# Moving an identity product one step later, with two PSUM banks given fixed names, in an edge-gated graph layer

## The chip, the cores and the metric

One Trainium2 chip, one core of it. The time is the device time of the whole program in microseconds (us). The kernel before was timed three times: 1103.55, 1104.61 and 1106.3 us, median 1104.61 us. One more execution was recorded by the hardware profiler; every duration of a single instruction comes from that one.

## The reference

`x` holds 16 graphs' node features (16 x 1024 x 256), `adj` is one sparse 1024 x 1024 matrix of edge weights, the same for all 16 graphs. For every graph:

```python
pre_u  = x @ W1[:256]                 # one row for each source node u
pre_v  = x @ W1[256:]                 # one row for each target node v
S      = sigmoid(relu(pre_u[:, :, None] + pre_v[:, None] + b1) @ W2 + b2)
a_t    = einsum('buv,bud->bvd', S * adj, x)
m_t    = einsum('uv,bud->bvd', adj, x) * x
z      = beta1 * x + beta2 * (a_t @ Wa + ba) + beta3 * (m_t @ Wm + bm)
```

Only the edges that `adj` really has are worked on. The output has the shape of `x`.

## The kernel before, in words

**Blocks and steps.** A block `k` is 128 target nodes of 4 graphs (8 node tiles times 4 groups of graphs: 32 blocks). Its edges are sorted into 10 lists of up to 128, five for each half of the 128 targets; one list is one step, so a block has `T = 10` steps and the program 320. The main loop (L886) runs over `n = 0 .. 321`, with `k, s = divmod(n, T)`: `s` is the step within the block. "Step 3" below means `s == 3`.

**What one edge list goes through.** GpSimd fetches, by an indirect DMA from a table in DRAM, the rows of the list's source nodes: `pre_u` and `x` of 4 graphs (L541, eight buffers `fetched`). TensorE spreads the targets' `pre_v` over the edges with a 0/1 matrix: `expand(n)`, two matmuls `pc<-X,mark` (L630). The PSUM tile `pc` has two buffers. VectorE adds the two (`add`, L665) and does relu, the product with W2 and the sum, once for each of the 4 graphs (`gate`, L673, with the accumulator read behind each). ScalarE makes the sigmoid (L676) and the weighted 0/1 matrices `left` (L678, L640). TensorE sums up over the edges: `aggregate(n)`, `acc<-fetched,left` (L690). Step `n` of the loop issues, in this order: VectorE's add for `n + 1`, its gate for `n`, and `expand(n + 2)`. The aggregates are issued two steps' worth at once, in the odd steps, for `n - 3` and `n - 2`.

**What is done once for a block, spread over steps.** Step 8, step 9, and steps 0 and 2 of the next block: `turn_over` (L700) transposes a quarter of the sums into a PSUM tile (`misc<-ident_r,ev`, L708) and ScalarE copies it into `LT` (L711). Steps 4 to 7 of the next block: `block_end` (L727) multiplies by Wa (steps 4 and 6, behind a matmul that writes the bias, L454) and by Wm (steps 5 and 7), and ScalarE copies the sum out (L744). Steps 1 and 3: the products of the next block's targets with W1[256:] (`L454` for b1, then eight matmuls L450 `misc<-w_v,hT`), two of the 4 graphs in each step; they become `X`, which the next block's `expand` needs from step 8 on.

**The two ways of making X.** `halves` (L496) splits `pre_v` into a rounded part and a rest on VectorE. `halves_turned` (L481), used for `turned(k)`, that is for blocks 2 to 11 and 24 to 31 (18 of 32), does it in PSUM: ScalarE writes the rounded, negated product into `X[:, 0]` (L489) and copies its upper half (L490); then a matmul with the identity adds that rounded part to the same PSUM tile `p`, so that the rest is left there (L492, the *identity product*); then two ScalarE instructions (L494) write the rest into `X`. So `p` stays occupied from its products until L494 is done. The generator is resumed by `go(parts, n)`: at the end of steps 1 and 3 for the products (L861), at the head of steps 3 and 5 for the identity products (L888).

**PSUM.** `pc` takes four banks, `acc0` and `acc1` one each. The other two are the pool `psm` (L219), two buffers under one name: every other PSUM tile comes from `small()` (L221) and gets one of the two; the tile allocated before in that bank must have been read to the end.

**What else lies on the way.** In blocks 0 to 4 `rows` (L457) makes the `pre_u` rows of group 1 (eight matmuls L450 `misc<-w_u,hT` for half of a tile, a copy L466, a DMA to the table one step later); `plan` (L801) says at which steps the tile's x is loaded and the two halves are made, and `rows` for groups 2 and 3 is planned further on. Until step 110 the edge lists of the tiles 4 to 7 are made by the generators `lists` (L243); their stages that use TensorE and a bank of `psm` say `"step"` and are put by `piece_of` and `fill` (L646, L657) between the other work, outside steps 1 to 6.

**Order.** The order of TensorE, VectorE, ScalarE, GpSimd and SyncE is the order in which the Python issues instructions (L515); each engine works through its own list in that order. The only freedom is how far one engine runs ahead of another.

Of the kernel before, what the change touches and what calls it, by code (L numbers as in the profile page):

```python
# [7 lines left out]
FP = mybir.dt.float32  # L8
# [5 lines left out]
P = 128  # L14
# [3 lines left out]
def kernel(  # L18
# [43 lines left out]
    B, N, D = x.shape  # L62
    NT = N // P
# [96 lines left out]
    same = hv.rearrange("p w q one -> p (w q) one").to_broadcast([P, NW * Q, V])  # L160
# [19 lines left out]
    slot, nth = upto, upto[:, :S]  # L180
# [26 lines left out]
    main = ctx.enter_context(ExitStack())  # L207
# [8 lines left out]
    lst = lst.enter_context(tc.tile_pool(name="lst", bufs=1))  # L216
    psc = main.enter_context(tc.tile_pool(name="psc", bufs=2, space=bass.MemoryType.PSUM))
    psa = main.enter_context(tc.tile_pool(name="psa", bufs=1, space=bass.MemoryType.PSUM))
    psm = main.enter_context(tc.tile_pool(name="psm", bufs=2, space=bass.MemoryType.PSUM))  # L219

    def small(name):  # L221
        return psm.tile([P, 512], FP, name="misc")


    def aside(vt):
# [17 lines left out]
    def lists(vt):  # L243
# [22 lines left out]
        cut = lst.tile([P, 1], FP, name="cut", bufs=2)  # L266
        nc.vector.tensor_reduce(cut, cand[:, :, 7], AX.X, ALU.max)
        yield "op"
# [93 lines left out]
        k_of = lst.tile([P, M], FP, name="k_of", bufs=2)  # L362
        nc.vector.tensor_reduce(k_of, eq, AX.X, ALU.add)
        yield "op"
# [33 lines left out]
    def count_rest():  # L398
        most = const.tile([P, 1], FP, name="most")
        nc.vector.tensor_reduce(most, longest, AX.X, ALU.max)  # L400
        nc.vector.tensor_copy(turns[:, :NT], longest)
# [45 lines left out]
    def half_product(p, hT, wt, h, begun):  # L447
        for bb in range(2):
            for i in range(DC):
                nc.tensor.matmul(p[:, bb * D:(bb + 1) * D], hT[:, 2 * h + bb, i, :], wt[:, i, :],  # L450
                                 start=(i == 0 and not begun), stop=(i == DC - 1), skip_group_check=begun)

    def add_row(p, parts):
        nc.tensor.matmul(p, unit, parts.unsqueeze(1).to_broadcast([P, 2, D]),  # L454
                         start=True, stop=False, skip_group_check=True)
# [22 lines left out]
    def turned(k):  # L478
        return 2 <= k <= 11 or k >= 24

    def halves_turned(k):  # L481
        X = cuts[k] = big.tile([P, NW, GD], FR, name="X")
        for h in range(2):
            yield
            c = slice(2 * h * D, (2 * h + 2) * D)
            p = small("p")
            add_row(p, b1_p)
            half_product(p, hTs[order[k]], w_v, h, True)
            nc.scalar.activation(X[:, 0, c], p, AF.Copy, scale=-1.0)  # L489
            nc.scalar.copy(X[W:, 1, c], X[W:, 0, c].bitcast(FP))  # L490
            yield
            nc.tensor.matmul(p, ident_r, X[:, 0, c], start=False, stop=True, skip_group_check=True)  # L492
            for w in range(NW):
                nc.scalar.activation(X[(1 - w) * W:(2 - w) * W, w, c], p[w * W:(w + 1) * W], AF.Copy, scale=-1.0)  # L494
# [23 lines left out]
    def do(step):  # L518
        for f in due.pop(step, ()):
            f()  # L520

    def go(gen, step):

        try:
            gen.send(step)
        except StopIteration:
            pass

    T = TW * NW

    BS = NG * NT
# [15 lines left out]
    def whole(pieces):  # L547
        return (said for said in pieces if said not in ("op", "slot"))

    made = [whole(lists(vt)) if vt < EARLY else lists(vt) for vt in range(NT)]  # L550
    turn = [(g, vt) for g in range(2) for vt in (*range(FIRST, NT), *range(FIRST))]
# [19 lines left out]
    def load_mark(q):  # L571
        marks[q] = big.tile([P, E], FR, name="mark")
        nc.scalar.copy(marks[q], whose[:, order[q // NW][1] * NW + q % NW, :])  # L573
# [9 lines left out]
    for t, turns_ in enumerate(script):  # L583
        step = t - 100
# [40 lines left out]
    def expand(n):  # L625
        k, g, vt, w, j = where(n)
        pcs[n] = psc.tile([P, GD], FP, name="pc")
        for h in range(2):
            c = slice(2 * h * D, (2 * h + 2) * D)
            nc.tensor.matmul(pcs[n][:, c], marks[n // TW][:, j * P:(j + 1) * P], cuts[k][:, w, c],  # L630
                             start=True, stop=True)
# [12 lines left out]
    running = []  # L644

    def piece_of(r, n):  # L646

        said = next(r[0], None)
        if said is None:
            running.remove(r)  # L650
        else:
            n += {"load": 4 if n else 7, "wait": 2, "slot": 1, "step": 1}.get(said, 0)
            while said == "step" and n > ROOM and 0 < n % T < 7:
                n += 1
            r[1:] = said not in ("slot", "step"), n

    def fill(n, gap=True):  # L657
        for r in running:
            if r[1] == gap and r[2] <= n:
                piece_of(r, n)  # L660
                break

    def add(n):
        t = fetched[at_slot[n]][:, :GD]
        nc.vector.tensor_tensor(t, t, pcs.pop(n), ALU.subtract if turned(n // T) else ALU.add)  # L665
# [126 lines left out]
    start_list = dict(zip((0, 14, 44, 72), range(EARLY, NT)))  # L792
    loads, at = {}, {}

    def plan(blocks, ns):

        for k, (load, *pieces) in zip(blocks, ns):
            loads[load] = k
            at.update((n, k) for n in pieces)

    plan(turn[NT:], ((0, 1, 8), (1, 9, 10), (9, 17, 18), (11, 19, 20), (19, 27, 28), (21, 29, 30), (29, 38, 39), (31, 40, 48)))  # L801
    for g, first in ((2, 60), (3, 140)):
        plan([(g, vt) for vt in range(NT)], ((first - 4 + 10 * i, first + 8 + 10 * i, first + (10 if first + 10 * i < 100 else 12) + 10 * i)
                                             for i in range(NT)))
# [62 lines left out]
    ROOM, MORE, LISTS = 10, 3, 110  # L867
# [9 lines left out]
    def gather_in(n):  # L877
        aggregate(n)
        free.append(at_slot.pop(n))
        refill()  # L880
        fetch_val(1 + (n % 3 == 0))
        if (n + 1) % TW in (0, MID + 1):
            half_end(n, 0 if (n + 1) % TW else 1)

    done = 0
    for n in range(total + 2):  # L886
        k, s = divmod(n, T)
        if s in (3, 5) and turned(k + 1) and k + 1 < BS:  # L888
            go(parts, n)
        if n < total - 3:  # L890
            last_in = n - 1 if n % 2 or n < ROOM else done
        else:
            last_in = n
        while done < min(last_in, total):
            gather_in(done)
            done += 1
        if n % TW == 1 and n // TW + 1 < total // TW:
            load_mark(n // TW + 1)
        if n < ROOM:
            if n + 2 < total:  # L900
                expand(n + 2)
            products(n, k, s)
        if n + 1 < total:
            add(n + 1)
        if n < total:
            gate(n)
            if n + 1 < total:
                left_adj(n + 1)
        do(n)
        if n >= ROOM and n + 2 < total:  # L910
            expand(n + 2)
        if n == 1:
            w_a = load_weights(Wa, "w_a", nc.sync)
            w_m = load_weights(Wm, "w_m", nc.sync)
            bias = load_rows(bm, D, "bias", nc.sync, spare[:, 1])
            ba_b = load_rows(ba, D, "ba_b", nc.sync, spare[:, 2])
            be1 = load_rows(beta1, 1, "be1", nc.sync)
            be2 = load_rows(beta2, 1, "be2", nc.sync)
            be3 = load_rows(beta3, 1, "be3", nc.sync)
            after(10, scale_late)  # L920
        if s in (5, 7) and k < BS - 1:
            h = s // 7
            hb = big.tile([P, 2, D], FP, name="h_blk", bufs=4)
            hbs.setdefault(k, []).append(hb)
            g, vt = order[k]
            nc.sync.dma_start(hb.rearrange("p b d -> p (b d)"),
                              table[g][vt * P:(vt + 1) * P, GD + 2 * h * D:GD + (2 * h + 2) * D])
        if n == total - 6:
            hbs[BS - 1] = hT_free.pop(0).rearrange("p b c n -> p b (c n)")
            for v, m, f in tails:  # L930
                for h, o in tail_rows(x, v, m, f):
                    nc.sync.dma_start(h, o)
        for i in advance.get(n, ()):
            next(made[i], None)
        if n in start_list:
            running.append([made[start_list[n]], True, n])
            piece_of(running[-1], n)
        fill(n, False)
        if n >= ROOM:
            products(n, k, s)  # L940
        if n == LISTS:
            assert not running and all(next(x, None) is None for x in made)
            lists_done()
            more = main.enter_context(tc.tile_pool(name="more", bufs=1))
            hT_free.extend(hT_places(more, MORE, NH))
        if n == 120:
            nc.gpsimd.partition_all_reduce(longest, rest, P, bass_isa.ReduceOp.max)
            after(n + 12, count_rest)
# [7 lines left out]
    with tc.If(any_left > 0):  # L956
        with ExitStack() as s2:
# [4 lines left out]
            for vt in range(NT):  # L962
# [17 lines left out]
                f = fb.tile([P, 2 * GD], FP, name="fb_f")  # L980
# [83 lines left out]
```

## Time and profile before

| | before |
|---|---|
| median of 3 runs | 1104.61 us |
| profiled execution: its time | 1116.06 us |
| its span, first to last instruction | 1114.2 us |
| around the span | 1.9 us |
| mean granted TensorE clock | 0.971 |
| TensorE (PE) busy | 1031.7 us |
| ScalarE (ACT) busy | 864.2 us |
| identity products (L492) | 36, mean 556 ns, 23.7 us of waits before them |
| L494 | 72, mean 592 ns |
| L489, L490 | 36 each, mean 588 ns and 616 ns |

PE is TensorE's matmuls, PEld its weight loads, DVE is VectorE, ACT is ScalarE, POOL is GpSimd, SP is SyncE. An instruction line of the timeline gives start, duration, engine, source line, operation, output and input with partitions x elements, how many are merged into the line, and in brackets the idle time of the engine just before and what ended it. Matmuls overlap in the pipeline: of two lines of PE, the distance of the starts is what the first one took of the engine.

### The profile page before, as it was taken

Reading aid. Unit: us, or ns where it says so; the run is one execution under the profiler, and the core shown is the slowest. Engines: PE = TensorE matmul, PEld = TensorE weight load, DVE = VectorE, ACT = ScalarE, POOL = GpSimd, SP = SyncE. Lnnn points to the kernel's source line nnn. Section 1 sums busy time; section 2 is a strip of 40 time slices with the busy share of each in tenths; the row PEclk is TensorE's granted clock in tenths of the full one; section 3 lists DMA queues with packets and bytes.
Section 4 is the critical chain, followed back from the end, with each engine's and each line's share of the span. In section 5 each row is a group of like instructions: output and inputs, shape, how many; then the busy total and the mean of one; then the engine's idle time right before and its main releaser. Section 6 shows DMA issues by size and latency. Waiting matters only on the chain.

```text
span 1114.2 us, 23979 instructions
## 1 busy us (share of the span) xinstructions
PE 1031.7 (93%) x7681; PEld 735.3 (66%) x7681; DVE 1006.8 (90%) x3469; ACT 864.2 (78%) x2639; POOL 460.8 (41%) x453
## 2 busy tenths in 40 slices
PE   7777898998999999899999999999999999999996
PEld 6654566765576667677677767676766666666663
DVE  8788887999999999899999999999999999999993
ACT  3346676777788888788898888988898888888873
POOL 2746643764346325634333434334333323333320
PEclk9979999998999999999999999999999999999999
DMA  9999998999999999999999999999999999998991
GB/s 286 335 379 335 312 323 282 397 343 374 340 373 377 384 382 371 357 387 382 404 409 389 404 384 388 388 402 392 348 374 359 354 328 337 350 368 333 341 352 42
DMA packets 149032, 394.56 MB, mean 354 GB/s; under 512 B 18224, under 2 KB 96048, under 8 KB 112688
## 3 DMA queue, kind: packets, MB, share of 16 engines
q0 software_dynamic: 50240, 300.11, 69.7%
q1 hardware_dynamic: 85360, 79.71, 22.5%
q10 hardware_dynamic: 13296, 13.11, 3.5%
q8 instruction: 63, 1.03, 0.4%
q14 instruction: 73, 0.60, 0.1%
HBM read 396.93 MB, written 50.33 MB: 401 GB/s over the span
## 4 chain that ended last, share of the span: by engine, by line
PE 55%; DVE 23%; ACT 12%; issue 7%; another core or an unknown queue 1%; DMA 1%; DVEq 0%; ACTq 0%
PE acc L690 14%; PE misc L739 13%; PE misc L450 12%; DVE fetched L673 12%; PE pc L630 9%; DVE fetched L665 7%; ACT left L678 4%; PE misc L708 2%; PE misc L454 2%; ACT mark L573 1%; ACT gt L676 1%; ACT LT L711 1%; ACT left L640 1%; ACT ev L698 1%; PE misc L492 1%
## 5 line engine op out<-in xcount | busy, mean ns | idle before, releaser
L541 POOL DMA_INDIRECT fetched<-table,uidx x320 | 342.7, 1071 | 557.8 <-PE acc L690 366.0
L673 DVE SCALAR_TENSOR_TENSOR fetched<-fetched,w_b 128x256 f32<-128x256 f32 x1280 | 476.9, 419 | 0.0
L665 DVE TENSOR_TENSOR fetched<-fetched,pc 128x1024 f32<-128x1024 f32 x320 | 388.5, 1214 | 62.1 <-PE pc L630 39.9
L678 ACT ACTIVATE left<-left,gt 128x32 f32<-128x32 f32 (+1 forms) x1280 | 299.5, 304 | 10.4
L690 PE MATMUL acc<-fetched,left 128*32 128x256 f32 x4096 | 268.0, 392 | 3.0 <-issue 1.6
L630 PE MATMUL pc<-X,mark 128*128 128x512 f32 x640 | 247.0, 467 | 7.3 <-DVE fetched L665 5.6
L690 PEld LDWEIGHTS acc<-fetched,left 128*32 128x32 f32 x4096 | 121.5, 111 | 108.4 <-issue 42.0
L630 PEld LDWEIGHTS pc<-X,mark 128*128 128x128 f32 x640 | 107.4, 192 | 85.5 <-issue 48.8
L676 ACT ACTIVATE gt<-sc,b_b 128x4 f32<-128x4 f32 x320 | 95.2, 298 | 79.4 <-DVE fetched L673 68.1
L739 PE MATMUL misc<-w_m,LT 128*128 128x256 f32 x496 | 119.1, 383 | 0.0
L739 PE MATMUL misc<-w_a,LT 128*128 128x256 f32 x496 | 117.2, 379 | 0.0
L450 PE MATMUL misc<-w_v,hT 128*128 128x256 f32 x448 | 110.3, 391 | 0.0
L739 PEld LDWEIGHTS misc<-w_m,LT 128*128 128x128 f32 x496 | 95.1, 192 | 15.5
L739 PEld LDWEIGHTS misc<-w_a,LT 128*128 128x128 f32 x496 | 93.8, 189 | 15.3 <-issue 0.3
L640 ACT ACTIVATE left<-onehot,val 128x64 f32<-128x64 bf16 (+1 forms) x320 | 102.9, 322 | 0.0
L673 DVE DVE_READ_ACCUMULATOR fetched<-fetched,w_b 128x1 f32 x1280 | 101.6, 79 | 0.0
L390 POOL DMA_INDIRECT val<-in_adjT_dram,vidx x80 | 87.7, 1096 | 32.4 <-issue 20.4
L450 PEld LDWEIGHTS misc<-w_v,hT 128*128 128x128 f32 x448 | 88.8, 198 | 14.8
L698 ACT COPY ev<-acc 128x512 f32<-128x512 f32 x128 | 74.7, 584 | 26.2 <-PE acc L690 13.9
L708 PE MATMUL misc<-ident_r,ev 128*128 128x128 f32 x512 | 78.9, 277 | 16.7 <-ACT low L506 9.4
L708 PEld LDWEIGHTS misc<-ident_r,ev 128*128 128x128 f32 x512 | 61.5, 141 | 40.3 <-ACT low L506 14.2
L711 ACT COPY LT<-misc 128x512 f32<-128x512 f32 x128 | 73.2, 572 | 8.5 <-remote 5.0
(184 smaller groups left out, 972.2 us busy)
## 6 DMA issues: line engine op xcount, KB each, us to landing
h_blk<-table SPq DMA_DIRECT2D x62, 256.0 KB
out_dram<-h_blk SPq DMA_DIRECT2D x62, 256.0 KB
hT<-in_xT_dram SPq DMA_DIRECT2D x28, 512.0 KB
table<-in_x_dram ACTq DMA_DIRECT2D x24, 512.0 KB
table<-tab SPq DMA_DIRECT2D x48, 256.0 KB
fetched<-table,uidx POOLq DMA_INDIRECT x320
table<-in_x_dram SPq DMA_DIRECT2D x8, 512.0 KB
table<-fetched SPq DMA_DIRECT2D x8, 512.0 KB
```

The costliest lines, as they stand in the source:

```text
L390: nc.gpsimd.indirect_dma_start(out=val[:, i, j:j + 1], out_offset=None, in_=adj_flat, in_offset=bass.IndirectOffsetOnAxis(ap=vidx[:, i, j: ...
L450: nc.tensor.matmul(p[:, bb * D:(bb + 1) * D], hT[:, 2 * h + bb, i, :], wt[:, i, :], start=(i == 0 and not begun), stop=(i == DC - 1), skip ...
L541: nc.gpsimd.indirect_dma_start(out=fetched[at_slot[n]], out_offset=None, in_=table[g], in_offset=bass.IndirectOffsetOnAxis(ap=uidx[:, vt * ...
L630: nc.tensor.matmul(pcs[n][:, c], marks[n // TW][:, j * P:(j + 1) * P], cuts[k][:, w, c], start=True, stop=True)
L640: nc.scalar.activation(lefts[n][:, :m, 1::GB, :], onehot[:, i, o:o + m, :].unsqueeze(2).to_broadcast([P, m, GB // 2, V]), AF.Copy, scale=v ...
L665: nc.vector.tensor_tensor(t, t, pcs.pop(n), ALU.subtract if turned(n // T) else ALU.add)
L673: nc.vector.scalar_tensor_tensor(t[:, b, :], t[:, b, :], 0.0, w2_b, ALU.max, ALU.mult, accum_out=sc[:, b:b + 1])
L676: nc.scalar.activation(gt, sc, AF.Sigmoid, bias=b2_b)
L678: nc.scalar.activation(lefts[n][:, :m, 2 * b, :], lefts[n][:, :m, 1 + b // 2 * GB, :], AF.Copy, scale=gt[:, b:b + 1])
L690: nc.tensor.matmul(accs[h][b * 2 * V:(b + 1) * 2 * V, r, :], left[:, i, 2 * b - b % 2:2 * b - b % 2 + 2].rearrange("p k v -> p (k v)"), f[ ...
L708: nc.tensor.transpose(pt[:, r, :, c, :], ev[:, r, c * P:(c + 1) * P], ident)
L739: nc.tensor.matmul(pz[:, bb * D:(bb + 1) * D], LTs[k][:, 2 * h + bb, i if bb else 1 - i, c, :], wt[:, c, :], start=False, stop=(i == 0 and ...
```

## The change

`small()` alternates between two names, `misc0` and `misc1`, each with one buffer, instead of leaving the choice of the bank to the pool; the second half's products of `halves_turned` ask for the name used last, which is that of the transpositions of step 2. Both identity products are issued behind both halves' products: the first at the head of step 4 instead of step 3, the second at the head of step 5 as before. The stages of `lists` that use a bank are held off steps 1 to 6 at the moment they would be issued, instead of when they become ready. The plan of the `rows` of group 1 is moved: no half is made in step 7 any more, the last one comes at step 50 instead of 48.

```diff
-    psm = main.enter_context(tc.tile_pool(name="psm", bufs=2, space=bass.MemoryType.PSUM))
-
-    def small(name):
-        return psm.tile([P, 512], FP, name="misc")
+    psm = main.enter_context(tc.tile_pool(name="psm", bufs=1, space=bass.MemoryType.PSUM))
+    bank = 0
+
+    def small(name, same=False):
+        nonlocal bank
+        bank ^= not same
+        return psm.tile([P, 512], FP, name=f"misc{int(bank)}")
...
     def halves_turned(k):
         X = cuts[k] = big.tile([P, NW, GD], FR, name="X")
+        ps = []
         for h in range(2):
             yield
             c = slice(2 * h * D, (2 * h + 2) * D)
-            p = small("p")
+            p = small("p", h == 1)
+            ps.append(p)
             add_row(p, b1_p)
             half_product(p, hTs[order[k]], w_v, h, True)
             nc.scalar.activation(X[:, 0, c], p, AF.Copy, scale=-1.0)
             nc.scalar.copy(X[W:, 1, c], X[W:, 0, c].bitcast(FP))
+        for h, p in enumerate(ps):
             yield
+            c = slice(2 * h * D, (2 * h + 2) * D)
             nc.tensor.matmul(p, ident_r, X[:, 0, c], start=False, stop=True, skip_group_check=True)
             for w in range(NW):
                 nc.scalar.activation(X[(1 - w) * W:(2 - w) * W, w, c], p[w * W:(w + 1) * W], AF.Copy, scale=-1.0)
...
-            while said == "step" and n > ROOM and 0 < n % T < 7:
-                n += 1
-            r[1:] = said not in ("slot", "step"), n
+            r[1:] = said not in ("slot", "step"), n, said == "step"
...
-            if r[1] == gap and r[2] <= n:
+            if r[1] == gap and r[2] <= n and not (r[3] and n > ROOM and 0 < n % T < 7):
...
-    plan(turn[NT:], ((0, 1, 8), (1, 9, 10), (9, 17, 18), (11, 19, 20), (19, 27, 28), (21, 29, 30), (29, 38, 39), (31, 40, 48)))
+    plan(turn[NT:], ((0, 1, 8), (1, 9, 10), (9, 18, 19), (11, 20, 28), (20, 29, 30), (29, 38, 39), (31, 40, 48), (40, 49, 50)))
...
-        if s in (3, 5) and turned(k + 1) and k + 1 < BS:
+        if s in (4, 5) and turned(k + 1) and k + 1 < BS:
             go(parts, n)
```

More of the change, by code (lines that the diff above doesn't have):

```diff
@@ L935 @@
         if n in start_list:
-            running.append([made[start_list[n]], True, n])
+            running.append([made[start_list[n]], True, n, False])
             piece_of(running[-1], n)
```

## The prediction

> **What bounds the kernel now.** I read the busy shares first, then the waits, then one late block as a table by stretches and as a timeline engine by engine.
>
> ```profile
> PE 1031.7 (93%) x7681; PEld 735.3 (66%) x7681; DVE 1006.8 (90%) x3469; ACT 864.2 (78%) x2639; POOL 460.8 (41%) x453
> ```
> Three engines are nearly full, so the bound lies in how they wait for each other. The waits, all engines:
>
> ```profile
> DVE fetched L665 <- PE pc L630: 39.9, 50, 2.1
> ...
> PE misc L492 <- ACT X L489: 23.7, 15, 2.8
> ```
> TensorE's largest wait, 23.7 us, stands before the identity product; the change is aimed at it. Which block it costs what is seen in block 27 (late, with no lists and no rows in it). One period of it, by stretches (busy us by engine):
>
> ```profile
> 943.81:973.07 29.26, 27.31 (x219) 18.98 (x218) 27.89 (x95) 25.31 (x81) 10.13 (x10) 1.00 0.96 348
> ```
> VectorE has 27.89 us of work in 29.26: it idles 1.37, nearly all in one place. TensorE's timeline of steps 2 to 5:
>
> ```profile
> 952.63 0.64 PE L708 MATMUL misc<-ident_r,ev 128*128 128x128 f32 x4
> 955.15 0.50 PE L492 MATMUL misc<-X,ident_r 128*128 128x512 f32 x1 [1.88 <-ACT X L489]
> 955.58 1.50 PE L690 MATMUL acc<-fetched,left 128*32 128x256 f32 x24
> 957.01 0.73 PE L630 MATMUL pc<-X,mark 128*128 128x512 f32 x2
> 957.82 0.50 PE L454 MATMUL misc<-b_p,unit 128*128 128x512 f32 x1
> 958.16 1.89 PE L450 MATMUL misc<-w_v,hT 128*128 128x256 f32 x8
> 959.70 0.81 PE L630 MATMUL pc<-X,mark 128*128 128x512 f32 x2
> 960.34 0.39 PE L454 MATMUL misc<-bias_p,unit 128*128 128x512 f32 x1
> 960.57 1.89 PE L739 MATMUL misc<-w_a,LT 128*128 128x256 f32 x8
> 962.11 0.58 PE L492 MATMUL misc<-X,ident_r 128*128 128x512 f32 x1
> 962.62 1.93 PE L690 MATMUL acc<-fetched,left 128*32 128x256 f32 x32
> 964.48 0.74 PE L630 MATMUL pc<-X,mark 128*128 128x512 f32 x2
> ```
> ScalarE and VectorE over the same time:
>
> ```profile
> 957.20 0.56 ACT L711 COPY LT<-misc 128x512 f32<-128x512 f32 x1
> 957.79 1.20 ACT L494 ACTIVATE X<-misc 64x512 fp32r<-64x512 f32 x2
> ...
> 960.40 0.60 ACT L489 ACTIVATE X<-misc 128x512 fp32r<-128x512 f32 x1
> 961.03 0.61 ACT L490 CAST X<-X 64x512 fp32r<-64x512 f32 x1
> ```
> ```profile
> 965.26 1.22 DVE L665 TENSOR_TENSOR fetched<-fetched,pc 128x1024 f32<-128x1024 f32 x1 [1.35 <-PE acc L690]
> ```
> Three things are to be seen. First, the second half's products start at 957.82, 0.06 after the copy L711 of step 2's transposition ends (957.76), and while L494 still reads the first half's tile (to 958.99): they already lie in the transpositions' bank. Naming the bank changes nothing. Second, the wait of 1.88 hides behind that: without it, these products still could not start before 957.76. Third, from there TensorE runs without a gap to the expand of step 5, ending at 965.22, and VectorE has waited 1.35 us for it. So one loop sets the period: gates on VectorE, ScalarE up to L711, TensorE from the second half's products to that expand, VectorE again. What lengthens the stretch 957.82 to 965.22 lengthens the block.
>
> **The change, part by part.**
>
> *Identity product from the head of step 3 to step 4, late blocks.* Removed: the wait of 1.88 and 0.43 of TensorE (955.15 to 955.58) in step 3. Two things are late next. The second list's aggregate needs `left`, ready at 954.38 (the four L678 that ScalarE began at 953.42); with 1.0 for its 16 matmuls and 0.57 for the expand TensorE gets to the products at about 956. There it waits for L711 until 957.76. Nothing is gained.
>
> Added in step 4, on the same clock. The products run 957.82 to 960.05 as before; TensorE takes the identity product at 959.70 (0.51, as 962.11 to 962.62), the expand at 960.21 (0.64), and could begin the Wa products (L454 at 960.34 above) at 960.85. But the bank was the transpositions' for the second half, so Wa's is the first half's, now held until its L494 pair has read it. ScalarE issues that pair behind the second half's L489 and L490: queued L489 (0.60), L490 (0.61), L494 (1.20), gaps 0.05. ScalarE is free at 960.05, since L494 no longer stands ahead of step 3's gate. So: 960.05 + 0.05 + 0.60 + 0.61 + 1.20 + 0.05 + 0.06 = 962.6. The wait is 1.75 to 1.8, and Wa starts 2.3 late (0.51 identity, 1.8 wait). Behind it TensorE has the second identity product, 32 aggregates and the expand that VectorE waits for: it ends at 967.5 instead of 965.22, VectorE's stall grows from 1.35 to 3.65, the period from 29.26 to 31.55. Bounds for this new wait, which the trace does not show: 0 if ScalarE were through by 960.85, 2.4 if the whole chain of 2.4 were bare. I take 1.8. Sum: 8 blocks (23 to 30) x 2.3 = **+18.4**.
>
> *The same in blocks 1 to 10.* Products again start 0.05 or 0.06 after L711 ends (201.88 after 201.83, 338.46 after 338.40, 405.49 after 405.44), so 2.3 is added there too, 23 in ten blocks. Less: blocks 1 and 5, where the waits of 2.84 and 1.87 did delay the products (1.0 and 1.25 past L711; the first estimated from the gates); blocks 2 and 3, where VectorE has list work and takes the expand 1.0 and 0.8 after it is ready (169.32 against 168.31; 210.05 against 209.28). 23 - 4.05 = **+19**.
>
> *Rows out of step 7.* At steps 17 and 27 the row products wait for the copies of a list's tile: 1.64 (on L294) and 2.99 (on L350), and run slowly behind it (L450 2.50 and 3.33 instead of 1.89, the Wm products 3.11 and 2.29 instead of 1.89): 4.6 + 3.7 = 8.3 at most. At least 0, or a loss of 2 if four halves in steps 8 to 0 each wait up to 0.5 for the Wm copy's bank (L744, 0.48 to 0.59); a fetch already ends one VectorE wait near there (1.26 at 151). I take **-6**, nearest to the rows with a cause. The moved loads still lead their rows by nine steps (some 27 us); the last table half leaves SP at step 51 instead of 49, and the first fetch from group 1 (step 60) is issued at 55. No cost seen there.
>
> *Hold on the lists' stages.* Same steps barred, tested later: 0, at worst one bank wait of 1 to 3.
>
> *Clock.* The granted clock in the stretch 894.13 to 897.5, behind a wait of 1.88, is 0.70 and 1.00 before. Four of the eight late blocks have it: their period is 30.51, +1.25. Seven of the 18 blocks show it in all. After the change each block has two gaps of about 1.8. None cold: -9; as often per block as late blocks now: +2.5; counted by gap: +14. I take **+5**.
>
> The Trainium skill, "TensorE: Matmul & The Clock Gate", section "HAM oscillation — how this bites in real kernels", asks only that no gap exceed some 3.4 us. By that rule the clock would cost nothing, here or before; the rows above show half-speed behind 1.88, so I go by them.
>
> The skill's "Perfetto Trace Analysis", section "Matmuls", says that independent groups should rotate through PSUM banks so that one's evacuation overlaps the next one's matmuls. It speaks against this change: two open halves take both banks at once.
>
> Sum: 18.4 + 19 - 6 + 5 = +36. The profiled execution, 1116.06 (span 1114.2 plus 1.9 around it), becomes 1152. It lies 11.5 over the median of the runs; the differences are the same there: 1104.6 + 36 = **1141 us**.
>
> **Rivals.**
>
> *Faster: the wait was the bound.* If L494 were done before TensorE gets to Wa, VectorE's stalls in step 6 go: 1.35 x 8 late blocks, about 1 x 10 early ones, 6 for the rows: 1104.6 - 27 = 1078. For it: the chain of waits that ended last does pass through L492 (955.15). Against: L711's end. It decides where ScalarE needs under 0.8 from the products' end (960.05) to L494's end; the rows give 2.4.
>
> *Absorbed early.* If the early blocks have slack everywhere (lists on VectorE, fetches), only the late ones pay and the rows give 8.3: 1104.6 + 18.4 - 8.3 = 1115. For it: blocks 2 and 3. Against: in blocks 6 to 10 VectorE waits 1.1 to 1.5 for the same expand.
>
> *Clock worse.* Both gaps make TensorE cold in every block: 36 x 1.25 less 7 x 1.25 = +36 in place of +5: 1172.
>
> **How the numbers follow.** Forecast 0.78 (1118 to 1160: per block 1.5 to 2.4, rows -8 to +2, clock -5 to +14), absorbed 0.08, faster 0.08, clock worse 0.06. The range 1112 to 1162 takes in the absorbed case. About 0.3% (3.3 us) is what a measurement can tell: faster 0.08, within 0.03 (part of the absorbed case), slower 0.89.
>
> **What would show it.** Right: L492's wait on L489 gone; waits of 1.7 on L711 before L454 in step 3 and 1.8 on L494 in step 4; late blocks at 31.5; VectorE's stall before L665 near 3.6 a block. Wrong: L454 in step 4 starting within 0.7 of the expand before it, or late periods under 29.3. The prediction fails if ScalarE does L494 ahead of the second half's L489.

## The result and the profile after

| | before | after |
|---|---|---|
| median, 4 runs each, same chip (us) | 1105.03 | 1138.2 (1135.78 to 1142.47) |
| ratio to before, with its 95% interval | | 1.0305 [1.027, 1.0339] |
| profiled execution: time, span (us) | 1116.06, 1114.2 | 1137.42, 1135.6 |
| mean granted TensorE clock | 0.971 | 0.980 |
| late block, shortest period (us) | 29.26 | 31.47 |

The change costs 33.2 us. The two profiled executions are only 21.4 us apart: before's lay 11 us above its median, over half of it from a late start (its first targets' products of step 1 in block 1 begin at 110.15; after's at 103.78, and those of the other kernels profiled between 102.9 and 104.9). That is not the change's doing, so medians give the size below and the profiles only the place. Ratios, here and below, go by the executions in the faster of two states alone, so a ratio need not be the quotient of the medians beside it.

In the new kernel the lines have moved: the bias product L454 is now L457, the identity product L492 is L499, its two ScalarE instructions L494 are L501, L489 and L490 are L494 and L495, the copy L711 is L716, the Wa and Wm products L739 are L744, VectorE's add L665 is L670. Busy time of after, from the top of its page:

```profile
PE 1031.6 (91%) x7681; PEld 731.1 (64%) x7681; DVE 1007.3 (89%) x3469; ACT 863.7 (76%) x2639; POOL 462.4 (41%) x453
```

No engine has noticeably more work than before (PE 1031.7, DVE 1006.8, ACT 864.2, POOL 460.8); the loss is waiting. The waits of after (who waited, for whom; total us, times, longest):

```profile
DVE fetched L670 <- PE pc L637: 87.3, 52, 4.1
...
PE misc L457 <- ACT X L501: 29.9, 18, 1.7
PE misc L457 <- ACT LT L716: 26.5, 18, 3.1
```

The identity product's 23.7 us of waiting on L489 have gone. In their place stand two waits in each of the 18 blocks: 29.9 / 18 = 1.66 on the first half's L501 in step 4, and 26.5 / 18 = 1.47 on the copy of step 2's transposition. VectorE's wait for the expand has grown from 39.9 to 87.3. TensorE in one late block, steps 3 to 5:

```profile
937.80 0.50 PE L457 MATMUL misc<-b_p,unit 128*128 128x512 f32 x1 [1.68 <-ACT LT L716]
938.14 1.89 PE L453 MATMUL misc<-w_v,hT 128*128 128x256 f32 x8
939.68 0.58 PE L499 MATMUL misc<-X,ident_r 128*128 128x512 f32 x1
940.10 0.63 PE L637 MATMUL pc<-X,mark 128*128 128x512 f32 x2
942.46 0.50 PE L457 MATMUL misc<-bias_p,unit 128*128 128x512 f32 x1 [1.74 <-ACT X L501]
...
946.71 0.73 PE L637 MATMUL pc<-X,mark 128*128 128x512 f32 x2
```

ScalarE over the same time:

```profile
937.18 0.56 ACT L716 COPY LT<-misc 128x512 f32<-128x512 f32 x1
...
940.07 0.60 ACT L494 ACTIVATE X<-misc 128x512 fp32r<-128x512 f32 x1 [0.30 <-PE misc L453]
940.70 0.61 ACT L495 CAST X<-X 64x512 fp32r<-64x512 f32 x1
941.22 1.19 ACT L501 ACTIVATE X<-misc 64x512 fp32r<-64x512 f32 x2
```

and VectorE's add for step 6, the instruction that the prediction followed:

```profile
947.48 1.22 DVE L670 TENSOR_TENSOR fetched<-fetched,pc 128x1024 f32<-128x1024 f32 x1 [3.61 <-PE pc L637]
```

Read them together. The second half's products start 0.06 after L716 ends (937.74), as they did after L711 before; the bank's name has bought nothing. The identity product and the expand pass through at once, and then TensorE stands from 940.72 to 942.46. ScalarE, from 940.07 on, does first the second half's L494 and L495, 1.15 us that the first half does not need, and only from 941.22 the L501 pair that frees the bank: the pair ends at 942.41, and L457 starts 0.05 later. The last expand ends at 947.44, and VectorE has waited 3.61 us for it where it waited 1.35. The period as a stretch, busy us by engine:

```profile
937.80:969.30 31.50, 28.09 (x219) 19.20 (x219) 27.87 (x97) 25.32 (x80) 10.04 (x10) 1.00 0.86 314
```

VectorE has 27.87 us of work in it, as before (27.89 in 29.26); the 2.24 us are added to its idle time.

### The profile page after: what moved, and what is told of

It reads as the page before. It is cut to its first block, busy times and chain, and to the rows that moved or that the text cites. A ratio compares the mean times of both kernels' runs of the same rounds, so it can differ in the third digit from the quotient of the medians.

```text
span 1135.6 us, 23998 instructions
## 1 busy us (share of the span) xinstructions
PE 1031.6 (91%) x7681; PEld 731.1 (64%) x7681; DVE 1007.3 (89%) x3469; ACT 863.7 (76%) x2639; POOL 462.4 (41%) x453
## 4 chain that ended last, share of the span: by engine, by line
PE 46%; DVE 22%; ACT 16%; DMA 9%; issue 6%; SPq 0%; POOL 0%; DVEq 0%; POOLq 0%; ACTq 0%
PE misc L744 13%; DVE fetched L678 11%; PE acc L695 11%; PE misc L453 10%; DVE fetched L670 8%; PE pc L637 6%; ACT left L683 4%; DMA table<-tab 4%; DMA fetched<-table,uidx 3%; PE misc L457 3%; ACT X L501 2%; ACT LT L716 2%; PE misc L713 1%; ACT X L495 1%; ACT gt L681 1%
## 5 line engine op out<-in xcount | busy, mean ns | idle before, releaser
L670 DVE TENSOR_TENSOR fetched<-fetched,pc 128x1024 f32<-128x1024 f32 x320 | 389.1, 1216 | 97.5 <-PE pc L637 87.3
L637 PE MATMUL pc<-X,mark 128*128 128x512 f32 x640 | 241.5, 459 | 9.4 <-DVE fetched L670 9.4
L744 PE MATMUL misc<-w_m,LT 128*128 128x256 f32 x496 | 117.6, 380 | 0.0
L744 PE MATMUL misc<-w_a,LT 128*128 128x256 f32 x496 | 117.2, 379 | 0.0
L453 PE MATMUL misc<-w_v,hT 128*128 128x256 f32 x448 | 114.2, 401 | 0.0
L744 PEld LDWEIGHTS misc<-w_a,LT 128*128 128x128 f32 x496 | 93.9, 189 | 14.6 <-ACT LT L716 0.4
L647 ACT ACTIVATE left<-onehot,val 128x64 f32<-128x64 bf16 (+1 forms) x320 | 102.9, 322 | 0.0
L744 PEld LDWEIGHTS misc<-w_m,LT 128*128 128x128 f32 x496 | 93.4, 190 | 14.6
L453 PEld LDWEIGHTS misc<-w_v,hT 128*128 128x128 f32 x448 | 90.8, 203 | 15.1
L716 ACT COPY LT<-misc 128x512 f32<-128x512 f32 x128 | 73.0, 571 | 3.0 <-PE misc L713 2.0
```

The lines of the kernel that those rows point to most:

```text
L647: nc.scalar.activation(lefts[n][:, :m, 1::GB, :], onehot[:, i, o:o + m, :].unsqueeze(2).to_broadcast([P, m, GB // 2, V]), AF.Copy, scale=v ...
L716: nc.scalar.copy(LT.rearrange("p b k c (r v) -> p r (b k c) v", v=V)[:, r:r + 2], pt.rearrange("p r k c v -> p r (k c) v"))
L744: nc.tensor.matmul(pz[:, bb * D:(bb + 1) * D], LTs[k][:, 2 * h + bb, i if bb else 1 - i, c, :], wt[:, c, :], start=False, stop=(i == 0 and ...
```

## The experiments

The ratios are to runs of the kernel before on the same chip, whose median was between 1102.8 and 1103.36 us in the three groups. "Early" is the stretch from the first targets' products of block 1 to those of block 11, "middle" from there to block 23, "late" from there to the second half's products in block 30.

| run | ratio [95%] | early, middle, late (us) | late period, shortest |
|---|---|---|---|
| before (its one profile) | 1 | 352.1, 368.4, 216.8 | 29.26 |
| after | 1.0305 [1.027, 1.0339] | 365.5, 365.3, 230.6 | 31.47 |
| e1 | 1.0018 [0.9985, 1.005] | 348.5, 364.5, 219.3 | 29.28 |
| e2 | 1.0325 [1.0261, 1.039] | | 31.49 |
| e3 | 1.0142 [1.008, 1.0204] | | 30.58 |
| e4 | 1.0572 [1.0497, 1.0646] | | 32.15 |
| e5 | 1.0052 [1.0021, 1.0083] | 346.7, 364.8, 221.1 | 30.05 |
| e6 | 0.9955 [0.9922, 0.9987] | 347.5, 364.8, 212.5 | 29.25 |
| e7 | 0.9931 [0.9904, 0.9957] | 335.5, 364.7, 213.0 | 28.91 |
| e11 | 0.9852 [0.9817, 0.9888] | 336.5, 368.3, 204.3 | 28.29 |
| e8 | 0.9896 [0.9859, 0.9933] | 342.9, 375.8, 204.2 | |
| e13 | 0.9998 [0.996, 1.0035] | 344.2, 365.9, 216.8 | 29.26 |
| e14 | 1.0023 [0.9995, 1.005] | 334.0, 391.9, 204.2 | |

The theory: the loss comes from the place of the identity products, through the bank that stays held behind ScalarE's queue. The rivals: the bank names, the new row plan, or the clock.

**e1: the identity products back, all else of the change kept.**

```diff
-        if s in (4, 5) and turned(k + 1) and k + 1 < BS:
+        if s in (3, 5) and turned(k + 1) and k + 1 < BS:
```
(and in `halves_turned` each half's identity product follows its own products again)

> The changed kernel with only the identity products put back to the heads of steps 3 and 5; bank names, lists' hold and row plan as changed. Theory (the first half's bank is held until ScalarE has read it behind the second half's copies, 2.3 us on the path of each of 18 blocks): all of the loss goes, and the row plan's gain of about 6 us shows: 1099 us, 1094 to 1106; late blocks 29.3 us apart again, no wait on L494's kind before the Wa products. Rival (strict alternation of two named banks or the moved rows cost it): it stays near 1138 us.

Measured 1104.78 us, ratio 1.0018 [0.9985, 1.005]. Names, hold and row plan together cost at most 0.5%, and the loss goes with the place. What was expected beyond that, a gain of some 4 us from the row plan, is not there. Late blocks are back at 29.3 us in one period of seven; in the other six they take 30.0 to 30.4, since six of the eight late blocks run partly at half the granted clock (last section).

**e2: the move alone.** The kernel before, with the split loop of `halves_turned` and steps (4, 5); the two-buffer pool, the old plan and the old hold stay.

```diff
-        if s in (3, 5) and turned(k + 1) and k + 1 < BS:
+        if s in (4, 5) and turned(k + 1) and k + 1 < BS:
```

> The kernel before with only the identity products moved behind both halves, to the heads of steps 4 and 5; the pool of two buffers chooses the banks, the row plan is the old one. Theory: the whole loss without the plan's gain, 1144 us (1138 to 1150); late blocks at 31.5 us; the pool chooses the same banks, so the same wait of about 1.75 us before the Wa products. Rival (names or plan make the loss): near 1105 us.

Measured 1141.95 us, ratio 1.0325 [1.0261, 1.039]: the whole loss, without one named bank. The waits of e2 are those of after (here L498 is the pair, L715 the copy):

```profile
PE misc L454 <- ACT X L498: 30.7, 18, 2.1
PE misc L454 <- ACT LT L715: 28.7, 18, 3.1
```

So the pool of two gives the second half the same bank by itself.

**e3: a shorter queue ahead of the release.** In the changed kernel the second half's rounded copy and its upper half are issued behind the first half's L501 pair (here L506) instead of ahead of it.

```diff
-            nc.scalar.activation(X[:, 0, c], p, AF.Copy, scale=-1.0)
-            nc.scalar.copy(X[W:, 1, c], X[W:, 0, c].bitcast(FP))
+            if h == 0:
+                rounded(p, c)
...
             for w in range(NW):
                 nc.scalar.activation(X[(1 - w) * W:(2 - w) * W, w, c], p[w * W:(w + 1) * W], AF.Copy, scale=-1.0)
+            if h == 0:
+                rounded(ps[1], slice(2 * D, 4 * D))
```
(`rounded(p, c)` is a new function that holds the two lines taken out)

> The changed kernel, with the second half's two ScalarE instructions (rounded copy and its upper half, 0.60 and 0.61 us) issued behind the first half's pair of reads instead of ahead of it. Theory: the queue on ScalarE is the price; the pair ends 0.05 + 1.20 us after the identity product, so the wait before the Wa products falls from 1.75 to about 0.7 us and late blocks from 31.5 to 30.4: 1120 us (1115 to 1126). Rival (the place of the identity product itself on TensorE is the price, 0.5 us and cold clock): no change, 1138 us.

Measured 1122.04 us, ratio 1.0142 [1.008, 1.0204], period 30.58. ScalarE and then TensorE of e3, late block:

```profile
936.88 1.19 ACT L506 ACTIVATE X<-misc 64x512 fp32r<-64x512 f32 x2 [0.52 <-PE misc L504]
938.10 0.60 ACT L489 ACTIVATE X<-misc 128x512 fp32r<-128x512 f32 x1
```
```profile
938.12 0.50 PE L457 MATMUL misc<-bias_p,unit 128*128 128x512 f32 x1 [0.82 <-ACT X L506]
```

The pair now starts as soon as the identity product has ended, and the wait falls from 1.74 to 0.82 with no work removed from ScalarE. What is left is the pair itself (1.19) less the part of the expand that runs beside it. Half of the loss was order on ScalarE; the other half is the identity product and its pair lying between two uses of one bank.

**e4: a longer queue.** The second half's upper-half copy is issued twice (the same data, a second time), so that 0.62 us more stand ahead of the pair.

```diff
-            nc.scalar.copy(X[W:, 1, c], X[W:, 0, c].bitcast(FP))
+            for _ in range(1 + h):
+                nc.scalar.copy(X[W:, 1, c], X[W:, 0, c].bitcast(FP))
```

> The changed kernel with the upper-half copy of the second half issued twice (0.62 us more on ScalarE ahead of the first half's pair of reads, same data). Theory: the wait before the Wa products grows by 0.62 us to about 2.35 in each of 18 blocks and late blocks to 32.1: 1149 us (1144 to 1153). Rival (ScalarE has room, 76% busy): no change, 1138 us.

Measured 1166.7 us, ratio 1.0572 [1.0497, 1.0646]. TensorE of e4 in a late block:

```profile
930.39 0.50 PE L457 MATMUL misc<-bias_p,unit 128*128 128x512 f32 x1 [2.39 <-ACT X L502]
930.73 3.51 PE L745 MATMUL misc<-w_a,LT 128*128 128x256 f32 x8
```

The wait is 1.74 + 0.65 = 2.39, and the one late period of seven in which the clock stays up is 32.15, 0.65 longer, as the queue's length says. But the other six are 33.75 to 35.48: at half the granted clock behind the gap of 2.39 the eight Wa products take 3.51 instead of 1.89. The direction and the wait were right; the size missed since the clock was left out of it.

**e5: the row plan alone**, in the kernel before.

```diff
-    plan(turn[NT:], (... (9, 17, 18), (11, 19, 20), (19, 27, 28), (21, 29, 30), (29, 38, 39), (31, 40, 48)))
+    plan(turn[NT:], (... (9, 18, 19), (11, 20, 28), (20, 29, 30), (29, 38, 39), (31, 40, 48), (40, 49, 50)))
```

> The kernel before with only the new plan of group 1's rows (none in step 7). The prediction gave the plan -6 us; the first run with the identity products put back showed no gain. Theory now: the two waits of step 7 go, but a table half is needed again two steps after its last use (steps 18 and 20, 38 and 40, 48 and 50), and ScalarE waits there for the DMA of the old one (2 to 6 us seen at three places): 1103 us, 1099 to 1107, waits of ScalarE's row copy on the table's DMA of 5 us or more in all. Rival (the plan gains and the bank names or the lists' hold cost the same): 1097 us.

Measured 1107.59 us, ratio 1.0052 [1.0021, 1.0083]: a loss of 5 us where a gain was expected. Two waits of e5 that before has not:

```profile
ACT tab L466 <- DMA table<-tab: 13.7, 3, 7.4
...
PE misc L454 <- ACT tab L466: 11.0, 4, 5.3
```

Each half of a table row has one buffer in SBUF, and the transfer out of it took a median of 8.6 us from issue to landing, over the 12 of 48 whose landing the trace has. ScalarE waits 5.80 us before the half of step 20, which begins 12.4 us after the copy of step 18 into the same buffer ended, and 7.36 us before the last half at step 50, which begins 13.4 us after that of step 48 ended. The changed kernel waits 2.61 and 3.23 us at the same two places. In before six halves also follow two steps behind their buffer's last use, 6.8 to 9.7 us after that copy ended, and none waits for a transfer. Without the waits e5's two would have come after 6.6 and 6.0 us: the plan brings them somewhat closer, but these two transfers were also slower than any of the six.

That these waits are the loss is not shown. In the profiled execution of e5 the early stretch (346.7) is no longer than that of e6 (347.5), which has the old plan; the late stretch, in which the plan does nothing, is 4.3 us longer than before's, with seven late blocks of eight partly at half the clock where before has four.

**e13: the same plan, the transfer issued at once** instead of a step later.

```diff
-                after(step + 1, lambda t=t, c=c: nc.sync.dma_start(table[g][nt * P:(nt + 1) * P, c], t))
+                nc.sync.dma_start(table[g][nt * P:(nt + 1) * P, c], t)
```

> The kernel before with the new row plan, as in the run of the plan alone, but each half's DMA to the table is issued in the step that made it instead of one step later, some 3 us sooner. Theory: the plan's gain was eaten by ScalarE waiting for that DMA before it may overwrite the table half (13.7 us in three waits); sooner DMAs cut these to about 5 us, and the plan's own gain comes out: 1097 us (1093 to 1102). Rival (the plan loses elsewhere, or to the clock): as the plan alone, about 1107 us.

Measured 1105.72 us, ratio 0.9998 [0.996, 1.0035]. It misses its figure, and its edit moved nothing in time: SyncE, which issues these transfers, stands ready for them in both kernels. In e5 the transfer of step 48's half is issued at 242.15, 0.02 us after the copy's end at 242.13; in e13 at 236.18, 0.02 after 236.16; all 16 halves of group 1 have 0.02 or 0.03 in both. So the expectation's "some 3 us sooner" did not come about, and this run does not test how much of e5's loss is the wait for the transfer.

What it shows is how much such transfers vary. The wait before step 20 has gone: the transfer of step 18's half landed 5.5 us after its issue. But 8.61 us stand before the last half, since the transfer of step 48's half landed only after 15.1 us; from the end of the copy to the next use of its buffer it is 15.2 us here (236.16 to 251.32) and 13.4 in e5 (242.13 to 255.50). As a second measurement of the plan it says, with e1, that the plan gains no 6 us; whether it costs 5 or nothing stays open. A second buffer for each half, which would tell, was not tried.

**e6: the wait of 1.88 removed without holding a bank longer.** In the kernel before, the first identity product is issued behind step 3's aggregates instead of ahead of them.

```diff
-        if s in (3, 5) and turned(k + 1) and k + 1 < BS:
+        if s == 5 and turned(k + 1) and k + 1 < BS:
             go(parts, n)
...
+        if s == 3 and turned(k + 1) and k + 1 < BS:
+            go(parts, n)
```

> The kernel before with the first identity product still in step 3, but behind the step's aggregates instead of ahead of them. TensorE then does not stand 1.88 us at the identity product. Theory (the second half's products are gated by ScalarE's copy of step 2's transposition, so that wait was free): no gain from it, late blocks stay at 29.3 us, the wait comes back before these products (about 1.5 us); 1103 us, 1098 to 1107, a few us lower at most if the split gap leaves the clock up. Rival (the wait at the identity product was on the path): 1.3 us less per block, 1080 us.

Measured 1098.32 us, ratio 0.9955 [0.9922, 0.9987]. TensorE of e6, late block:

```profile
939.03 0.50 PE L492 MATMUL misc<-X,ident_r 128*128 128x512 f32 x1
939.36 0.62 PE L630 MATMUL pc<-X,mark 128*128 128x512 f32 x2
941.44 0.50 PE L454 MATMUL misc<-b_p,unit 128*128 128x512 f32 x1 [1.45 <-ACT LT L711]
```

The identity product waits for nothing, and the second half's products wait for L711 instead. The period is 29.25 to 29.29 in every late block: not 0.05 shorter than the clean one of before. The 4.5 us that are gained are those of the blocks that were cold (partly at half the granted clock): the late stretch is 4.3 us shorter than before's, as much as before's seven late periods lie above the clean one (4.3), and no late block of e6 is cold, behind a gap of 1.45.

**e7: the other gate alone.** The transposition of step 2 goes to the head of step 2, ahead of the gather of step 2, in the turned blocks; the identity product keeps its place and its wait.

```diff
+        if s == 2 and 0 < k < BS and turned(k + 1) and n >= ROOM:
+            turn_over(k - 1, 1, 1, n)
```
(and it is left out at its old place there)

> The kernel before with the transposition of step 2 and its copy issued at the head of step 2 in the 18 blocks, so that ScalarE copies it ahead of step 2's gate; identity products as before. Theory: the gate of the second half's products opens 1.4 us earlier, but TensorE, held at the identity product, gets there only 0.24 us earlier: late blocks about 29.0, 1098 us (1094 to 1103). Rival (the transposition's copy is no gate): no change or slower by TensorE's earlier wait for the copy of the sums, 1104 to 1115.

Measured 1093.28 us, ratio 0.9931 [0.9904, 0.9957]; period 28.91. L492's wait on L489 is still 19.8 us in all, so in late blocks little is gained until that goes too. The time lies just below the range that was expected. The early blocks gain more than the late ones: 335.5 us against 347.5 in e6 and 352.1 in before. What they gain it from was not followed up.

**e11: e6 and e7 together**, in the kernel before.

> Both edits of the two runs beside it: first identity product behind step 3's aggregates, transposition of step 2 at the head of the step; old plan, pool of two buffers. Theory: only together do they open the stretch, because each alone leaves the other's wait: TensorE reaches the second half's products 1.1 us earlier and finds the bank free, VectorE's stall of 1.35 falls to about 0.4, late blocks 28.3; 18 blocks x 1.0 and up to 7 x 1.25 of clock: 1080 us (1074 to 1090). Rival (effects add): 1098 us.

Measured 1085.59 us, ratio 0.9852 [0.9817, 0.9888], the fastest of all kernels here. TensorE and VectorE of e11 in a late block:

```profile
927.75 0.50 PE L492 MATMUL misc<-X,ident_r 128*128 128x512 f32 x1
928.09 0.62 PE L630 MATMUL pc<-X,mark 128*128 128x512 f32 x2
928.75 0.50 PE L454 MATMUL misc<-b_p,unit 128*128 128x512 f32 x1
```
```profile
936.58 1.22 DVE L665 TENSOR_TENSOR fetched<-fetched,pc 128x1024 f32<-128x1024 f32 x1 [0.33 <-PE pc L630]
```

Neither gate is left, and VectorE's stall, 1.35 before and 3.61 after, is 0.33. The late period shows that the gates lay beside each other: e6 takes 0.01 off it, e7 0.35, both 0.97. The whole time alone would hardly show it: the ratios of e6 and e7 multiply to 0.9886, inside the upper edge of e11's interval.

**e8: e11 with the new row plan.**

> Both edits in the 18 blocks, with the new row plan instead of the old one. Theory (the plan swaps two waits for a list's copy against three waits for the table's DMA): within 5 us of the run with both edits and the old plan, 1085 us (1080 to 1091). Rival (the plan costs nearly 5 us, as it did alone): 1090 us.

Measured 1092.78 us, ratio 0.9896 [0.9859, 0.9933], above the expected range and nearest to the rival's figure, though its interval overlaps e11's. In the profiled execution the early stretch is 342.9 us instead of 336.5, and ScalarE waits 18.9 us for the table's transfers (three times, 12.43 the last). The middle stretch is longer too, 375.8, with one wait of 9.8 on a load in it, so not all of the difference between the two profiles is the plan's.

**e14: e11 with the early transposition in all blocks**, the twelve middle ones with the other way of making X among them (`k + 1 < BS` for `turned(k + 1)`).

> As the run with both edits (identity product behind step 3's aggregates, step 2's transposition at its head), the early transposition now in all blocks from 1 on, the twelve with the other way of making X too. There a row product in step 2 and the transposition behind it stand before banks that ScalarE still reads (9.4 us in 12 waits). Theory: 0.5 to 1 us less in each of those blocks: 1077 us (1070 to 1084). Rival (those blocks are bound by TensorE's work alone): as with both edits in 18 blocks, about 1085 us.

Measured 1104.34 us, ratio 1.0023 [0.9995, 1.005]: all of e11's gain is gone, in the middle stretch alone (391.9 instead of 368.3). TensorE of e14 there:

```profile
574.46 1.99 PE L450 MATMUL misc<-w_u,hT__6481 128*128 128x256 f32 x8 [1.87 <-ACT low L506]
```

The transposition took the free bank, and the row products of step 2 now take the one that ScalarE is still reading for the first half's X: 22.4 us of waits in twelve blocks (in e11 the small transposition stood there, with 6.9 us in eleven waits). The expectation did not look at what is issued next for the bank: the change's own fault once more.

## Why the prediction was right, and which terms were not

It said 1141 and slower; it is 1138.2, and the wait that it worked out is the one that the runs show as the cause. By its own steps:

- **"Naming the bank changes nothing"**: shown by e2, which has the loss without the names.
- **The wait in step 4, 1.75 to 1.8**: measured 1.74, in the order and at the places of the sum (pair ends 942.41, Wa starts 942.46). e3 and e4 move it with the queue ahead of the pair, down to 0.82 and up to 2.39.
- **Late blocks, 2.3 each, 31.55**: measured 2.24 and 31.50; VectorE's stall 3.61 for 3.65. Over the late blocks and the end of the program the profiles differ by 17.5 us (13.8 in the late stretch, 3.7 behind it), for 18.4 without the clock.
- **Early blocks, +19**: against e1, which differs from after only in this move, the early stretch is 365.5 - 348.5 = 17.0 us longer.
- **"Nothing is gained" from the wait of 1.88**: right for the period (e6: 29.25). It left out that the same gap let the clock fall; without it e6 gains 0.45% [0.13%, 0.78%].
- **Rows out of step 7, -6**: wrong, there is no gain. e5 has +0.52% [0.21%, 0.83%], e13, whose transfers were issued at the same moments, -0.02% [-0.4%, 0.35%], and e1, with all but the move, +0.18% [-0.15%, 0.5%]; -6 us would be -0.54%. The step that failed is "No cost seen there": it followed the loads and the first fetch, and not the buffer that a half shares with the one two steps ahead of it. The 8.3 us of waits and slow products at steps 17 and 27 were real rows (they give 4.8 and 3.5, the same sum as the prediction's 4.6 and 3.7), but e5 shows no gain from their going. Whether the new waits are what took the gain stays open.
- **Clock, +5**: wrong in sign, small. Over seven late periods the excess over the clean period was 4.3 us before and 2.7 after, and the mean granted clock is higher after: 0.979 to 0.983 in its four timed executions, 0.966 to 0.979 in those of before. Two gaps of 1.7 in a block made TensorE cold in three late blocks of eight, one of 1.88 in four of eight. The term went by how often a gap of that length was followed by half the clock; the last section shows that the place of the gap decides too. The rival in which every block goes cold did not happen to this change; it nearly did in e4.

That the sum came this close is partly luck. The move alone costs 32 to 36 us (after against e1; e2 against before), where its terms had 18.4 + 19 + 5 = 42.4; the row plan, which had -6, gained nothing. The two errors nearly cancel.

The other rivals are excluded: ScalarE needs 2.38 us from the end of the second half's products (940.03) to the end of the pair (942.41), where "faster" needed under 0.8, and the early blocks do not absorb the wait.

## What to carry to other kernels

Before removing the largest wait of an engine, find what would let the next instruction go if that wait were gone: here a copy ended 0.06 us ahead of what came next, and in the late blocks taking away the wait or the copy's lateness alone took 0.01 and 0.35 us off the period, both together 0.97. A PSUM bank held open for a second product costs all that stands ahead of its release in the reading engine's queue, so move the release ahead, and look at every later request for that bank, also when other work is moved in front of it. A buffer's next use has to be counted in landing times of its transfer, not in steps, when a plan is shifted.

## What the runs showed of the hardware that was not expected

The granted clock changes on a grid. In before the clock of four late blocks falls to half at 895.47, 926.19, 1014.94 and 1045.66, which lie 9, 26 and 9 times 3.41 us apart, and it stays there for 3.41 us each time. Three neighbouring stretches of the grid (TensorE's busy time comes first, the granted clock third from the end):

```profile
892.06:895.47 3.41, 1.53 (x23) 0.76 (x25) 3.41 (x11) 3.28 (x12) 0.00 (x0) 1.00 1.01 425
895.47:898.88 3.41, 3.41 (x18) 2.15 (x11) 3.41 (x11) 3.34 (x12) 1.98 (x2) 0.50 0.97 373
898.88:902.30 3.42, 3.42 (x17) 2.97 (x16) 3.03 (x13) 2.39 (x8) 0.00 (x0) 1.00 0.97 393
```

The gap of 1.88 us ahead of L492 (892.25 to 894.13) lies in the first of them, and the second has half the clock. So the place of a gap on the grid counts, and not only its length. The late blocks of before, e1, e5 and e13 have 32 gaps of 1.84 to 1.88 us: 21 lie inside one stretch (to within 0.02 us), and in every one of these cases the next stretch had half the clock; 11 are cut by a boundary, by 0.12 us or more, and none of these was followed by it. That is why the same gap made four late blocks of eight cold in before and in e13, six in e1 and seven in e5. With other gaps: none of eight behind 1.45 us (e6), three of eight behind 1.68 and 1.74 (after), seven of eight behind mostly 2.39 (e4), but also two of eight behind 1.41 in e7, where a gap of 0.29 lies shortly ahead. In after most gaps of 1.68 and 1.74 that lie inside one stretch were not followed by it, so how little work in a stretch is too little is not settled by these rows.

In after a cold block took 1.25 to 1.4 us more than a clean one; in e4 mostly 1.6. A wait that looked free by the dependencies cost 0.45% [0.13%, 0.78%], and by e6's profile that was the clock.

The transfer of a table half (256 KB) took a median of 8.6 to 9.8 us from issue to landing, over the landings that the traces of e5, e13 and e8 have, but single ones differ widely: 5.5 us for step 18's half and 15.1 us for step 48's in e13. What held the slow ones is not settled.
